# Three-term features kept in the gates' operand tiles, the power written later, one half of a relu written earlier

## The chip, the cores and the metric

The kernel runs on one core of one Trainium2 chip. The metric is the device time of one execution in microseconds (us); the median of several executions is compared. One core has five engines with an instruction queue each, which work through their queues in order and wait for each other through semaphores: TensorE (PE; its weight loads are shown apart as PEld), VectorE (DVE), ScalarE (ACT), GpSimd (POOL) and SyncE (SP). Transfers between HBM and SBUF run on 16 DMA engines; SyncE, ScalarE and GpSimd issue them.

## What is computed

A stack of four graph layers over N = 3327 nodes with D = 64 features and one weighted adjacency matrix `adj` (3327 x 3327, float32). `LN` is a layer norm over the features without scale or bias, and each layer is added to x:

```
h = relu(LN(x))
x = x + relu(ggc(relu(ggc(h, adj)), adj))        # layer 0: two gated graph cells (GRU)
h = relu(LN(x))
x = x + (W_rank @ (h @ w1) + b1)                 # layer 1
h = relu(LN(x))
x = x + three hops of  (adj*adj) @ . @ W.T + b   # layer 2
h = relu(LN(x))
x = x + two hops of  tanh([adj @ x, x] @ W)      # layer 3

ggc(x, adj):  m = adj @ (x @ W); gi = m @ wih.T + bih; gh = x @ whh.T + bhh
              r = sigmoid(i_r + h_r); z = sigmoid(i_z + h_z); n = tanh(i_n + r * h_n)
              return (1 - z) * n + z * x

W_rank: mask = adj != 0; rank = cumsum(mask, axis=1); deg = rank[:, -1:]
        k = min(deg, 100); pos = rank - (deg - k); W_rank = mask * 0.5 ** (k - pos) where pos > 0
```

So there are eight propagations through the adjacency matrix, numbered k = 0 to 7: two plain ones (k = 0, 1), one with the ranked weights (k = 2), three with squared entries (k = 3, 4, 5) and two plain ones (k = 6, 7).

## The kernel before

**Tiling.** The nodes are padded to 26 blocks of 128. The transposed matrix is read in tiles: one block of 128 source nodes (q = 0 to 25) against a group of target columns. There are two groups, `GROUPS` (L56): group 0 has the chunks 0 and 1 (384 columns each, in two halves s = 0, 1 of the node range), group 1 the chunks 2 and 3 (384 and 512 columns). A tile is 768 KB for group 0 and 896 KB for group 1 and lands in one of `NBUF` = 20 slots (L119). The sums of a chunk gather in PSUM over 26 source blocks.

**Units.** The work is a list of units (k, c, t): propagation k, target chunk c, tile t. `joint` (L615) lists two successive propagations of one group together, so that most tiles are loaded once for both. The order is k = 0 of group 0; k = 0 and 1 of group 1; k = 1 and 2 of group 0; k = 2 and 3 of group 1; and so on. Between the tiles of k = 0 stand counting units, which sum the mask of a tile over the rows (L496).

**The written order.** All engines follow the order in which the program emits their instructions. `run` (L667) goes through the units. For unit i it first emits loads as far ahead as slots are free (`dead`, a first-in first-out list; a load stops when only `RESERVE` = 3 are left), then prepares masks and squares some units ahead (`PREPARE`, L76), expands units up to i + 3 (`expand`, L444: for k = 2 two pairs of matmuls L270, then L474 on VectorE or L476 on ScalarE), then emits pieces of masks (L426 on VectorE; with the first half also the row DMA L431 on GpSimd), then the matmuls of unit i (`propagate`, L533, matmuls L561). Work that follows a finished chunk is written as generators. Each `yield` of one names a number of us, and `spend` (L337) takes from it an estimate for each unit that was emitted (0.645 us for 384 columns of a plain unit; 0.32 and 0.48 us for the two parts of a ranked one); when nothing is left, the generator runs on to its next `yield`. These are places in an order and not waits. `finish` (L329) runs a generator to its end at once; `propagate` calls it where the features of a source chunk are wanted and `y[k][cs]` isn't set yet (L551).

**The parts that the change touches.**
- `layernorm_relu` (L761): L766 to L768 on VectorE, a yield, L773 to L775, the power L776 on GpSimd (variance to the power -0.5), a yield of 2.5, and L780 on VectorE, which writes the features h.
- `before_0` (L868) uses it for the first features. It is advanced by hand before `run` (L972): each of the four chunks is begun and advanced twice, in the order 0, 0, 1, 0, 1, 2, 1, 2, 3, 2, 3, 3. At its end y[0][c] is set; after a further yield the features are transposed (L739).
- `gru` (L796): `both[c]` is a tile of 1 KB a partition and block that holds, for the two halves s, features in one half of the partitions and messages in the other, as the operand of the gates' matmuls (L807). L832 to L834 on VectorE make the new state d. In cell 0 its relu goes back into `both`, one half of the partitions by ScalarE (L837), the other by VectorE (L838). Matmuls L722 then bring it back to nodes (`stacked_to_nodes`), and a copy L881 makes y[1][c].
- `in_three` (L844) splits the features of k = 2 into three bfloat16 terms (L856 on ScalarE, L858 on VectorE), 0.75 KB a partition and block. They lie in a slot taken for each group: `parts[1]` when the first chunk of group 1 comes, `parts[0]` at the first chunk of group 0. The slots come back at L566 and L573. Four small DMAs (L865, on GpSimd) put the last row of each block into `lasty`.

Between the cell of k = 1 and the end of k = 5, where features are written into it anew, nothing reads `both[c]`.

Of the kernel before, what the change touches and what calls it, by code (L numbers as in the profile page):

```python
# [10 lines left out]
BF16 = mybir.dt.bfloat16  # L11
I16 = mybir.dt.int16
AF = mybir.ActivationFunctionType
ALU = mybir.AluOpType
# [30 lines left out]
N, D = 3327, 64  # L45
P = 128
NB = 13
# [5 lines left out]
NC = 4  # L53
PARTS = (4, 5)
CWM = 512
GROUPS = [(0, 1), (2, 3)]  # L56
# [14 lines left out]
PLAIN, RANKED, SQUARED = range(3)  # L71
KIND = [PLAIN, PLAIN, RANKED, SQUARED, SQUARED, SQUARED, PLAIN, PLAIN]
# [6 lines left out]
SPECIAL = None  # L79
# [3 lines left out]
def chunk_of(b):  # L83
    return next(c for c, (b0, b1) in enumerate(CH[:NC]) if b0 <= b < b1)


def sources_of(*chunks):
    return [s * NB + b for c in chunks for s in range(2) for b in range(*CH[c])]


def upper(n):
    return slice(n * D, (n + 1) * D)
# [3 lines left out]
def kernel(  # L96
# [9 lines left out]
    nc = tc.nc  # L106
# [12 lines left out]
    slots = [const.tile([P, 2, GWM], F32, name=f"adj{i}") for i in range(NBUF)]  # L119
# [7 lines left out]
    both = [const.tile([P, 2, (b1 - b0) * P], F32, name=f"both{c}") for c, (b0, b1) in enumerate(CH[:NC])]  # L127
# [131 lines left out]
    def blocks(c):  # L259
        return CH[c][1] - CH[c][0]  # L260

    def width(c):
        return blocks(c) * P
# [39 lines left out]
    def groups(t):  # L303
        return t.rearrange("p b s d -> p (b s) d")
# [24 lines left out]
    def finish(c):  # L329
        while c in tasks:  # L330
            advance(c)
# [5 lines left out]
    def spend(us):  # L337

        for c in list(tasks):
            if c in tasks and c not in running:  # L340
                tasks[c][1] -= us
                if tasks[c][1] <= 0:
                    advance(c)
# [6 lines left out]
    dead = deque(range(NBUF))  # L350
# [129 lines left out]
            t.mask.free()  # L480
        return wide.bitcast(BF16)

    ranks_left = set(sources_of(*GROUPS[0]))
    counts = {}
    squared = {}

# [46 lines left out]
    def propagate(k, c, t, rhs, first, last):  # L533
        if k == COUNT:
            count(t, first, last)
            return
        w = width(c)
        if first:
            sums[k, c] = [take(sums=True) for _ in range(2 if k == 7 and c == PARTS[1] else 1)]
            sums[k, c] = [sums[k, c][0], sums[k, c][-1]]  # L540
        acc = sums[k, c]
        if t is SPECIAL:
            for ch in range(NC):
                if ch != c:
                    finish(ch)
            terms = [[lasty[:, h, i, :] for h in range(2)] for i in range(3)]
            rhs = [rhs, rhs]
        else:
            s, b = divmod(t.q, NB)
            cs = chunk_of(b)  # L550
            if y[k][cs] is None:  # L551
                finish(cs)
            terms = [[yk[:, b - CH[cs][0], s, :]] * 2 for yk in (y[k][cs] if KIND[k] == RANKED else [y[k][cs]])]
            rhs = [rhs[:, h, :] for h in range(2)]
            if KIND[k] != RANKED:
                t.used()
            if (k, c, t) in squared:
                squared.pop((k, c, t)).free()
        for n, yq in enumerate(terms):
            for h in range(2):  # L560
                nc.tensor.matmul(acc[h][1][h * D:(h + 1) * D, :w], yq[h], rhs[h], start=first and n == 0,  # L561
                                 stop=last and n == len(terms) - 1)
        if KIND[k] == RANKED and c == NC - 1 and t is not SPECIAL and chunk_of(t.q % NB) in GROUPS[0]:
            ranks_left.discard(t.q)
            if not ranks_left:
                dead.append(parts[0])  # L566
        if t is not SPECIAL and t.early and t.mask is None:
            make_mask(t, RANKED)
        spend(STREAM_US * w / CWM * (0.75 if KIND[k] == RANKED else 1.0))
        if last:  # L570
            begin(c, after[k](c, sums.pop((k, c))))
            if KIND[k] == RANKED and c == NC - 1:
                dead.append(parts[1])  # L573

    units = []

# [184 lines left out]
    def layernorm_relu(h, c, scale=None, pace=1.0, squares_on_scalar=False):  # L761
        n = 2 * blocks(c)
        v = groups(xchunk(c))
        st = work.tile([P, 4, 8], F32, name="st", bufs=4)
        xc = work.tile([P, 8, D], F32, name="t2")
        nc.vector.tensor_reduce(st[:, 0, :n], v, AX.X, ALU.add)  # L766
        nc.vector.tensor_scalar(st[:, 1, :n], st[:, 0, :n], 1.0 / D, None, op0=ALU.mult)
        nc.vector.tensor_tensor(xc[:, :n], v, st[:, 1, :n, None].to_broadcast([P, n, D]), ALU.subtract)  # L768
        yield 1.5 * pace
        if squares_on_scalar:  # L770
            nc.scalar.activation(groups(h), xc[:, :n], AF.Square)
        else:
            nc.vector.tensor_tensor(groups(h), xc[:, :n], xc[:, :n], ALU.mult)  # L773
        nc.vector.tensor_reduce(st[:, 2, :n], groups(h), AX.X, ALU.add)
        nc.vector.tensor_scalar(st[:, 2, :n], st[:, 2, :n], 1.0 / D, EPS, op0=ALU.mult, op1=ALU.add)  # L775
        nc.gpsimd.tensor_tensor(st[:, 3, :n], st[:, 2, :n], mhalf[:, :n], ALU.pow)  # L776
        yield 2.5 * pace
        if scale is not None:
            nc.vector.tensor_scalar(st[:, 3, :n], st[:, 3, :n], scale, None, op0=ALU.mult)
        nc.vector.scalar_tensor_tensor(groups(h), xc[:, :n], 0.0, st[:, 3, :n, None].to_broadcast([P, n, D]),  # L780
                                       op0=ALU.max, op1=ALU.mult)
# [14 lines left out]
    def gru(acc, c, bi, bh, cell, pace=1.0):  # L796

        w = width(c)
        evacuate_stacked(acc, c)
        yield 0.8 * pace  # L800
        at = dead.popleft()
        r, z, d = (slots[at].rearrange("p s w -> p (s w)")[:, i * CWM:i * CWM + w] for i in range(3))

        def gate(g):
            i, ps = take()
            for s in range(2):
                nc.tensor.matmul(ps[upper(1 - s), :w], cells[:, cell, s, g, :], both[c][:, s], start=True, stop=True)  # L807
            return i, ps

        for g, v in enumerate((r, z)):  # L810
            i, ps = gate(g)
            nc.scalar.activation(v, ps[:, :w], AF.Sigmoid, bias=bsum[:, cell, g:g + 1])
            give(i)
        nh = None if cell == 0 else gate(2)
        ni = gate(3)
        yield 1.0 * pace
        nc.vector.scalar_tensor_tensor(r, ahead[c] if nh is None else nh[1][:, :w], bcol[:, bh + 2:bh + 3], r,
                                       op0=ALU.add, op1=ALU.mult)
        nc.vector.tensor_tensor(r, r, ni[1][:, :w], ALU.add)
        give(ni[0])  # L820
        if nh is not None:
            give(nh[0])
        else:
            del ahead[c]
            if not any(ch in ahead for ch in GROUPS[c // 2]):
                rooms[c // 2].free()
        yield 1.0 * pace
        nc.scalar.activation(r, r, AF.Tanh, bias=bcol[:, bi + 2:bi + 3])
        yield 0.8 * pace
        for s in range(2):  # L830
            u = upper(1 - s)
            nc.vector.tensor_tensor(d[u], both[c][u, s], r[u], ALU.subtract)  # L832
        nc.vector.tensor_tensor(d, d, z, ALU.mult)
        nc.vector.tensor_tensor(d, d, r, ALU.add)  # L834
        yield 2.2 * pace
        if cell == 0:
            nc.scalar.activation(both[c][upper(1), 0], d[upper(1)], AF.Relu)  # L837
            nc.vector.tensor_scalar(both[c][upper(0), 1], d[upper(0)], 0.0, None, op0=ALU.max)  # L838
            yield 1.0 * pace
        return at, d  # L840

    parts = {}

    def in_three(h, c):  # L844

        g = c // 2
        if g not in parts:
            parts[g] = dead.popleft()
        n = blocks(c) * 2 * 3 * D
        first = 2 * 3 * D * blocks(GROUPS[g][0]) if c == GROUPS[g][1] else 0  # L850
        room = slots[parts[g]].bitcast(BF16).rearrange("p s w -> p (s w)")[:, first:first + n]
        room = room.rearrange("p (b s i d) -> p b s i d", s=2, i=3, d=D)
        terms = [room[:, :, :, i, :] for i in range(3)]
        for i in range(2):
            yield 0.8
            nc.scalar.copy(terms[i], h)  # L856
            yield 0.8
            nc.vector.tensor_tensor(terms[2] if i else h, h, terms[i], ALU.subtract)  # L858

        yield 1.5  # L860
        b0, b1 = CH[c]
        for s in range(2):
            for k in range(2):
                q = k * D + s * NB
                nc.gpsimd.dma_start(out=lasty[q + b0:q + b1, k], in_=room[P - 1:P, :, s])  # L865
        return terms
# [155 lines left out]
```

## Time and profile before

Three executions took 719.84, 720.03 and 720.97 us; the median is 720.03 us. One more execution was profiled.

| what | value |
|---|---|
| median of the runs | 720.03 us |
| profiled execution, its own time | 723.89 us |
| its span, first to last instruction | 722.1 us |
| TensorE busy | 690.7 us, 96% of the span |
| VectorE busy | 346.2 us, 48% |
| ScalarE busy | 264.3 us, 37% |
| GpSimd busy | 77.3 us, 11% |
| moved by DMA | 201.31 MB, 279 GB/s over the span |
| TensorE idle before its first matmul | 8.4 us |

The profile page gives the busy time of each engine, the span in 40 slices, the DMA queues, the chain of work that ended last, and groups of instructions by line of the kernel with the idle time before them and what ended it. Further views of the same trace list waits, the instructions of an engine in order of time, the chain in order of time, and the granted clock of TensorE. Matmul ends are modelled, so a TensorE that shows busy is not always at its peak rate.

### The profile page before, as it was taken

To read this page: it belongs to the slowest core of one execution; us is meant where nothing else is said; L and a number is where in the kernel's file an instruction comes from. 1 tells how busy PE (TensorE), PEld (TensorE's weight loads), DVE (VectorE), ACT (ScalarE), POOL (GpSimd) and SP (SyncE) were. 2 spreads that over 40 slices of the span, in tenths; PEclk is the share of its full clock that TensorE was granted. 3 is DMA by queue.
4 is the path that set the end of the run, shared out by engine and by line. 5 is a ranking of instruction groups with operands and counts; after the bars stand their busy time and mean duration, and the time that the engine had idled before them with its cause. 6 is when DMAs were issued, how large, how long until landed. Compare 5 with 4: busy or idle time off the path is not lost.

```text
span 722.1 us, 12647 instructions
## 1 busy us (share of the span) xinstructions
PE 690.7 (96%) x5128; PEld 347.6 (48%) x5128; DVE 346.2 (48%) x701; ACT 264.3 (37%) x402; POOL 77.3 (11%) x114
## 2 busy tenths in 40 slices
PE   4999899999999897989999999999999999999997
PEld 1645444565446585445534444334444444344464
DVE  6767636634987987638615101521063456005101
ACT  0104000302137665778899321850065700000101
POOL 3500000001380602112100000000010000000000
PEclk9999999999999999999999999999999999999999
DMA  9999994299595367562799829981997399927991
GB/s 349 401 385 406 405 391 145 63 375 374 181 315 210 114 225 237 184 227 97 260 336 386 314 88 397 405 319 40 366 382 263 111 382 406 406 110 250 400 402 44
DMA packets 68549, 201.31 MB, mean 279 GB/s; under 512 B 7228, under 2 KB 8228, under 8 KB 68492
## 3 DMA queue, kind: packets, MB, share of 16 engines
q1 hardware_dynamic: 65596, 199.46, 74.6%
q8 instruction: 40, 0.66, 0.4%
q10 hardware_dynamic: 720, 0.85, 0.3%
q0 software_dynamic: 2176, 0.20, 0.2%
q14 instruction: 17, 0.14, 0.0%
HBM read 199.45 MB, written 0.85 MB: 277 GB/s over the span
## 4 chain that ended last, share of the span: by engine, by line
PE 52%; ACT 4%; DMA 2%; DVE 1%; issue 1%; ACTq 0%
PE sum L561 48%; ACT adj L403 3%; PE temp L270 3%; DMA adj<-totals 1%; PE temp L722 1%; DVE adj L426 1%; DMA out<-xs 1%; DVE both L757 0%; ACT both L756 0%; DVE xs L955 0%; ACT t L701 0%; PE sum L270 0%; ACT t L952 0%; ACT e L476 0%; ACTq L957 0%
## 5 line engine op out<-in xcount | busy, mean ns | idle before, releaser
L561 PE MATMUL sum<-adj,y 128*64 128x384 f32 (+3 forms) x3016 | 535.2, 505 | 12.1 <-DVE y L773 8.4
L561 PEld LDWEIGHTS sum<-adj,y 128*64 128x64 f32 x3016 | 223.3, 138 | 267.5 <-issue 223.8
L403 ACT ACTIVATE adj<-adj 128x768 f32<-128x768 f32 (+1 forms) x173 | 141.9, 891 | 50.2 <-PE sum L561 24.8
L426 DVE TENSOR_SCALAR adj<-adj 128x768 bf16<-128x768 f32 (+3 forms) x208 | 115.6, 606 | 32.4 <-PE temp L496 28.5
L476 ACT ACTIVATE e<-temp,bitsb 128x384 int16<-128x384 f32 (+1 forms) x114 | 65.4, 607 | 29.2 <-PE temp L270 16.1
L561 PE MATMUL sum<-e,adj 128*64 128x384 bf16 (+1 forms) x624 | 73.2, 341 | 0.6 <-DVE e L474 0.6
L757 DVE COPY both<-sum 64x384 f32<-64x384 f32 (+3 forms) x17 | 9.7, 568 | 117.1 <-ACT both L756 116.0
L756 ACT COPY both<-sum 64x384 f32<-64x384 f32 (+3 forms) x17 | 8.1, 478 | 154.8 <-PE sum L561 149.2
L270 PE MATMUL temp<-adj,tri 128*64 128x384 bf16 (+1 forms) x334 | 52.7, 348 | 8.7 <-DMA adj<-totals 5.4
L405 DVE TENSOR_TENSOR adj<-adj 128x768 f32<-128x768 f32 (+1 forms) x35 | 33.6, 1008 | 50.1 <-DMA adj<-in_adjT 29.6
L776 POOL TENSOR_TENSOR st<-st,mhalf 128x6 f32<-128x6 f32 (+1 forms) x16 | 24.5, 1531 | 295.5 <-DVE st L775 295.5
L561 PEld LDWEIGHTS <-adj 128*64 128x64 bf16 x624 | 40.3, 110 | 18.8 <-issue 6.7
L431 POOL DMA_DIRECT2D adj<-totals x52 | 31.4, 605 | 139.8 <-DVE adj L834 74.4
L474 DVE TENSOR_SCALAR e<-temp 128x384 int16<-128x384 f32 (+1 forms) x53 | 31.8, 607 | 26.3 <-issue 11.3
L270 PEld LDWEIGHTS <-tri 128*64 128x64 bf16 x416 | 28.9, 111 | 30.2 <-issue 13.7
L751 DVE STREAM_TRANSPOSE both<-y 32x96 f32<-32x96 f32 (+1 forms) x128 | 35.6, 278 | 2.9
L703 DVE COPY t<-sum 128x384 f32<-128x384 f32 x8 | 4.4, 555 | 62.2 <-PE sum L561 62.2
L496 PE MATMUL temp<-adj,behind 128*64 128x384 bf16 x208 | 29.1, 342 | 0.8 <-DVE adj L426 0.7
L496 PEld LDWEIGHTS <-behind 128*64 128x64 bf16 x208 | 14.1, 112 | 20.8 <-issue 18.6
L701 ACT COPY t<-sum 128x384 f32<-128x384 f32 (+1 forms) x8 | 4.2, 529 | 53.9 <-PE sum L561 53.9
L918 DVE TENSOR_TENSOR y<-temp,brow 128x384 f32<-128x384 f32 (+1 forms) x8 | 4.7, 592 | 29.6 <-PE temp L270 29.6
L530 ACT ACTIVATE lastw<-adj,bitsb 128x768 int16<-128x768 f32 (+1 forms) x2 | 2.0, 984 | 45.8 <-DVE adj L528 45.8
(121 smaller groups left out, 336.7 us busy)
## 6 DMA issues: line engine op xcount, KB each, us to landing
adj<-in_adjT SPq DMA_DIRECT2D x130, 768.0 KB, 8.7
adj<-in_adjT SPq DMA_DIRECT2D x104, 896.0 KB, 12.5
xs<-in_x SPq DMA_DIRECT2D x1, 640.0 KB, 4.0
adj<-totals POOLq DMA_DIRECT2D x26, 3.0 KB, 4.6
adj<-totals POOLq DMA_DIRECT2D x26, 3.5 KB, 3.1
out<-xs ACTq DMA_DIRECT2D x2, 192.0 KB
out<-xs ACTq DMA_DIRECT2D x1, 256.0 KB, 6.4
stage<-in_weights SPq DMA_DIRECT2D x2, 112.0 KB, 13.3
```

What stands on the lines that cost most here:

```text
L270: nc.tensor.matmul(out[hs], lhsT[:, hs], rhs, start=start, stop=stop)
L403: nc.scalar.activation(sq, v, AF.Square)
L405: nc.vector.tensor_tensor(sq, v, v, ALU.mult)
L426: nc.vector.tensor_scalar(t.mask.view[:rows, half], t.view()[:rows, half], 0.0, None, op0=ALU.not_equal)
L431: nc.gpsimd.dma_start(out=t.mask.view[P - 1:P], in_=totals[t.g][t.q:t.q + D + 1:D, :])
L474: nc.vector.tensor_scalar(wide[:, s], ps[:, :w], BITS, 0.0, op0=ALU.add, op1=ALU.max)
L476: nc.scalar.activation(wide[:, s], ps[:, :w], AF.Relu, bias=bitsb)
L496: nc.tensor.matmul(counts[c][1][s * D:(s + 1) * D, :w], behind[:, NQ - 1 - t.q:NQ - 1 - t.q + D], t.mask.view[:, s, t.cols(c)], start=firs ...
L561: nc.tensor.matmul(acc[h][1][h * D:(h + 1) * D, :w], yq[h], rhs[h], start=first and n == 0, stop=last and n == len(terms) - 1)
L751: nc.vector.transpose(to[at:at + 32, :, q], h[q * 32:(q + 1) * 32, :, s, f * 32:(f + 1) * 32])
L757: nc.vector.tensor_copy(both[c][upper(1), 1], acc[1][1][upper(1), :width(c)])
L776: nc.gpsimd.tensor_tensor(st[:, 3, :n], st[:, 2, :n], mhalf[:, :n], ALU.pow)
```

## The change

Three edits:
- **Terms in `both`.** `in_three` writes its three terms into `both[c]` in place of a slot. The two slots are no longer taken, and the code that gave them back is gone.
- **The power later.** In `layernorm_relu` a yield of 1.5 stands between L775 and the power, and one of 1.5 behind it, in place of 2.5 behind it alone. A layer norm thus has three yields, not two. The list that advances `before_0` by hand isn't changed.
- **Half of the relu at once.** In `gru`, cell 0, VectorE's half of the relu is written right behind L834, ahead of the yield; ScalarE's half stays behind it. The yield is 2.4 in place of 2.2.

```diff
-        if KIND[k] == RANKED and c == NC - 1 and t is not SPECIAL and chunk_of(t.q % NB) in GROUPS[0]:
-            ranks_left.discard(t.q)
-            if not ranks_left:
-                dead.append(parts[0])
...
             begin(c, after[k](c, sums.pop((k, c))))
-            if KIND[k] == RANKED and c == NC - 1:
-                dead.append(parts[1])
...
         nc.vector.tensor_scalar(st[:, 2, :n], st[:, 2, :n], 1.0 / D, EPS, op0=ALU.mult, op1=ALU.add)
+        yield 1.5 * pace
         nc.gpsimd.tensor_tensor(st[:, 3, :n], st[:, 2, :n], mhalf[:, :n], ALU.pow)
-        yield 2.5 * pace
+        yield 1.5 * pace
...
         nc.vector.tensor_tensor(d, d, r, ALU.add)
-        yield 2.2 * pace
+        if cell == 0:
+            nc.vector.tensor_scalar(both[c][upper(0), 1], d[upper(0)], 0.0, None, op0=ALU.max)
+        yield 2.4 * pace
         if cell == 0:
             nc.scalar.activation(both[c][upper(1), 0], d[upper(1)], AF.Relu)
-            nc.vector.tensor_scalar(both[c][upper(0), 1], d[upper(0)], 0.0, None, op0=ALU.max)
             yield 1.0 * pace
         return at, d
 
-    parts = {}
-
     def in_three(h, c):
 
-        g = c // 2
-        if g not in parts:
-            parts[g] = dead.popleft()
-        n = blocks(c) * 2 * 3 * D
-        first = 2 * 3 * D * blocks(GROUPS[g][0]) if c == GROUPS[g][1] else 0
-        room = slots[parts[g]].bitcast(BF16).rearrange("p s w -> p (s w)")[:, first:first + n]
+        room = both[c].bitcast(BF16).rearrange("p s w -> p (s w)")[:, :blocks(c) * 2 * 3 * D]
         room = room.rearrange("p (b s i d) -> p b s i d", s=2, i=3, d=D)
```

More of the change, by code (lines that the diff above doesn't have):

```diff
@@ L481, in expand @@
         return wide.bitcast(BF16)
-    ranks_left = set(sources_of(*GROUPS[0]))
     counts = {}
```

## The prediction

> **What bounds the kernel now.** I read the page first, then TensorE's waits, then for each long wait the instructions of the engine that it waited for. TensorE is the bound:
>
> ```profile
> PE 690.7 (96%) x5128; PEld 347.6 (48%) x5128; DVE 346.2 (48%) x701; ACT 264.3 (37%) x402; POOL 77.3 (11%) x114
> ```
>
> Only its 31.4 us of idle time (722.1 - 690.7) and what slows it can be won or lost. The view of waits for TensorE (who for whom: us, times, longest):
>
> ```profile
> PE sum L561 <- DVE y L773: 8.4, 1, 8.4
> PE temp L270 <- DMA adj<-totals: 5.4, 2, 3.3
> PE sum L561 <- DMA adj<-in_adjT: 2.8, 5, 1.4
> ...
> PE sum L722 <- DVE both L838: 2.1, 1, 2.1
> ```
>
> These four rows are the places that the change can reach: the start, two waits for a mask's last row, one for a tile, one for the relu. The start, VectorE in order of time:
>
> ```profile
> 3.17 0.55 DVE L766 TENSOR_REDUCE st<-xs 128x6 f32<-128x384 f32 x1 [3.17 <-DMA xs<-in_x]
> ...
> 4.56 0.56 DVE L773 TENSOR_TENSOR y<-t 128x384 f32<-128x384 f32 x1
> ...
> 5.82 0.55 DVE L766 TENSOR_REDUCE st<-xs 128x6 f32<-128x384 f32 x1
> ...
> 7.37 0.56 DVE L780 SCALAR_TENSOR_TENSOR y<-t,st 128x384 f32<-128x384 f32 x1 [0.21 <-POOL st L776]
> ```
>
> The first chunk's L780 starts at 7.37, and the first weight load follows 1.0 us later, at 8.37. VectorE around the relu:
>
> ```profile
> 71.76 0.56 DVE L834 TENSOR_TENSOR adj<-adj 128x384 f32<-128x384 f32 x1
> ...
> 76.18 0.34 DVE L838 TENSOR_SCALAR both<-adj 64x384 f32<-64x384 f32 x1
> ```
>
> The state is done at 72.32, but VectorE's half of the relu runs at 76.18, behind three mask pieces and the next chunk's state; TensorE, at L722 since 74.03, waits 2.13 us for it. GpSimd, and then the chain in order of time, around the two mask rows:
>
> ```profile
> 282.70 1.32 POOL L776 TENSOR_TENSOR st<-st,mhalf 128x6 f32<-128x6 f32 x1 [7.04 <-DVE st L775]
> 283.97 1.19 POOL L431 DMA_DIRECT2D adj<-totals  x2
> ```
> ```profile
> 283.97 4.42 DMA adj<-totals
> ...
> 317.10 5.18 DMA adj<-totals
> ```
>
> GpSimd sits in front of the power for 7.04 us; the row DMA behind it is issued at 283.97 and TensorE idles 3.33 us until it lands. The second row is issued only at 317.10 and costs 2.05 us.
>
> [...] The trace's clock record has three stretches at 0.5 of 3.41 us each, from 77.27, 288.89 and 323.02, right behind the waits of 2.13, 3.33 and 2.05 us[...], and none behind the tile wait of 1.36 us at 213.59. So a removed wait of 2 us or more brings 3.41 / 2 = 1.7 us beside itself. [...] a mask row issued at 291.32 with no tile on the way lands in 1.6 us, the two above in 4.4 and 5.2 us.
>
> **The change part by part.**
>
> *The start (the later power).* `before_0` now needs four advances to set y[0][c] and gets three. So before `run` VectorE gets L766 to L775 of all four chunks and no L780; the first unit finds y[0][0] unset, finishes the generator, and emits L780 and the six transposes L739 of chunk 0 ahead of its matmuls. VectorE: from 3.17, the first half (L766 to L768) takes 4.56 - 3.17 = 1.39 and the second (L773 to L775) 5.82 - 4.56 = 1.26, three times 2.65 = 7.95; the 512-wide chunk takes 1.64 + 1.52 by its own rows. L780 starts at 3.17 + 7.95 + 3.16 = 14.3, TensorE at 15.3: **6.9 us later**. Part of it comes back, since TensorE waits for tiles there: weight loads of successive tiles start at 42.80, 44.76, 46.68, 48.64, 50.63 and 52.56, 1.96 us apart, against 1.29 for 8 matmul records at 0.161 plus 0.32 for four counting ones. From 8.40 to 53.91 are 45.5 us; the work in it is 23 tiles x 1.29 = 29.7, 17 counts x 0.32 = 5.5, transposes 2.8, small matmuls 1.0, and 1.9 for the cold clock of the first 3.9 us: 40.9. The other 4.6 us are waits that a late TensorE doesn't have, its tiles having come meanwhile (loads don't wait for it: 17 tiles are issued by 26.6). 15.3 + 40.9 = 56.2 against 53.9, rounded up since it only just catches the last tiles: **+2.5** (bounds +1.5, and +6.9 if nothing comes back).
>
> *Relu at once.* L838 runs at 72.35. It adds nothing, but puts chunk 1's state 0.34 later. The wait of 2.13 and its 1.7 go; TensorE then comes to chunk 1's L722 at about 75.9, and ScalarE's half of it is done at 76.2: 0.3 back. **-3.5** (bounds -1.5, -3.8). The yield of 2.4 leaves chunks 0, 1 and 3 in the same unit; chunk 2 goes one unit later, and its copy L881 then meets the unit that reads it: at most 0.2.
>
> *The slots.* No slot is taken at chunk 2's L780, so each load of group 0's tiles 3 to 18 is issued at the place of the one before it. SyncE's issues were 202.20, 204.68 and 206.31 for the last three; the last now goes at 204.68, 1.6 us earlier, and lands when the one before it did, before TensorE's idle time began at 212.23. **-1.3** (bounds 0, -1.4). From the second slot on loads run two tiles ahead, but each still waits for the same slot to be read out, so they go at the same times. One place differs: the mask of tile 7 had the returned `parts[0]`; now it takes the slot that the load at 310.28 took. Its row goes at 310.3 in place of 308.14, and lands, 4 us later, before the 315.2 at which TensorE wants it; I put 0.3 on that. That load at 310.28 falls away (the tile is on its way already), and the row of 317.10 meets two tiles issued at 312.13 and 313.67, not three: 2.3 us less (896 KB at 406 GB/s), so it lands at about 320, when TensorE wants it (320.27). The wait of 2.05 falls to about 0.3 and the half clock with it: **-3.4** (bounds 0, -3.75).
>
> *The power at k = 2.* In group 0's second chunk L775 is emitted with unit (2,2,2) and the power 1.5 us of units later, with (2,2,13); the row DMA of tile 3 comes with the unit after next, (2,2,14), still behind it. GpSimd is held until 282.6 as before: **0** for the 3.33 us wait. Ahead of earlier powers some row DMAs and the clearing L518 now go first, but TensorE waited for none of them. L780 and the splits come one or two units later; VectorE is full from 231 to 250, and the same work passes through it: 0 (bounds -0.7, +0.7). The terms are read in the same shape from `both`: 0.
>
> *Sum.* +2.5 - 3.5 - 1.3 - 3.4 + 0.5 = -5.2, on a profiled span of 722.1, with 1.8 around it in that execution's 723.89. The runs' median is 3.9 below that execution; I take the same difference from it: 720.03 - 5.2 = **714.8 us**.
>
> **Rivals.**
> - *The slots win one wait of the two* (the tile, not the row: the row's slot is read out at 316.6 as before, and if its DMA still takes 5.2 us nothing is won): 714.8 + 3.4 = 718.2. *Neither*: 719.5.
> - *The start costs all of its 6.9*: if the late TensorE meets the tiles just the same. Against it, the 1.96 us pitch is a wait for tiles. 719.2.
> - *Relu moves the wait*: VectorE is full from 60 to 78, and the next chunk's half becomes the wait: -1.5 in place of -3.5, 716.8.
> - *The power does get behind the row of tile 3*, and the change does what its words say: 3.3 + 1.7 less, 709.8. Against it stands the count of units above.
> - *Slower: tiles ahead of rows.* If the deeper loads put one more tile of 2.3 us before each critical row: +2.3 at 288; tile 7's row, at 310.3 + 5.2 + 2.3 = 317.8, is 2.6 late plus 1.7; nothing won at 322. +2.5 - 3.5 - 1.3 + 2.3 + 4.3 + 0.5 = +4.8, 724.8. It decides once these rows cost over 3.5 us. For it, rows do wait behind tiles; against it, loads still follow slots.
>
> **How the numbers follow.** As summed 0.42; one slot wait alone 0.12; neither 0.08; full start 0.10; relu's wait moved 0.08; power past the row 0.10; slower 0.10. No change is within 0.2%, 1.4 us, about what these runs can tell: faster below 718.6, slower above 721.5. Faster: 0.42 + 0.12 + 0.08 + 0.10 = 0.72; same 0.08 + 0.10 = 0.18; slower 0.10. The range leaves out the two outermost cases, 0.10 each: 711.0 to 720.5; the likeliest alone has 712.5 to 717.
>
> **What would show it.** First matmul at about 15.3 and no tile waits before 55; no wait at L722 near 76 and no half clock there; no tile wait near 213; the wait at 288 still there, a power just before its row; no wait over 0.5 us near 320. A first matmul still at 8.4, a new wait for `totals` near 315, or a stretch at half clock that wasn't there would make it wrong.

## The result and the profile after

The changed kernel takes 718.04 us (median of 11 runs, 716.99 to 719.38) against 720.72 us for the kernel before beside it (11 runs). The medians are 2.7 us apart. The ratio on record, 0.9957 with a 95% interval of 0.9945 to 0.9970, is not that of these two medians; it makes 0.43%, 3.1 us (2.2 to 4.0). The forecast was 714.8 us and faster: the sign and the range (711.0 to 720.5) held, but the time lies outside the likeliest case's own range of 712.5 to 717: the gain came out at 3 us instead of 5.

The profiled executions say something else. Their spans are 722.1 us before and 716.2 us after, 5.9 us apart (5.2 were forecast on that scale). Why the profile shows nearly twice what the runs show is the main question below.

The changed kernel's page, first part (busy time of each engine):

```profile
PE 684.1 (96%) x5128; PEld 353.1 (49%) x5128; DVE 342.9 (48%) x700; ACT 265.3 (37%) x403; POOL 80.1 (11%) x114
```

TensorE is still the bound, with 32.1 us of idle time (716.2 - 684.1), 0.7 more than before. What fell is its busy time, by 6.6 us (690.7 to 684.1). Matmuls at half clock count as busy for longer here: before's L561 of 128x512 (f32) takes 1035 ns from 77.27 to 80.68 us, at a clock of 0.50, and 592 ns from 60 to 77. The three stretches at half clock of before, 3.41 us each, make 5.1 us of what fell. The changed kernel's trace has none of them ahead of its last matmul. Its waits after (in total, times, longest):

```profile
PE temp L732 <- DVE y L774: 15.0, 1, 15.0
PE temp L270 <- DMA adj<-totals: 3.1, 2, 2.5
...
PE sum L560 <- DMA adj<-in_adjT: 1.1, 1, 1.1
```

Against before, the start's wait grew from 8.4 to 15.0, the two waits for mask rows fell from 5.4 to 3.1, the tile waits from 2.8 to 1.1, and the relu's 2.1 is gone. The start in order of time, TensorE's row and then VectorE's:

```profile
14.96 1.55 PE L732 MATMUL temp<-ident,y 128*64 128x128 f32 x12 [14.96 <-DVE y L774]
```
```profile
14.36 1.49 DVE L774 SCALAR_TENSOR_TENSOR y<-t,st 128x384 f32<-128x384 f32 x3
```

All four chunks' first halves run first, and L774 (L780 before) is at 14.36, forecast at 14.3. VectorE around chunk 0's relu, and the one new wait behind it on TensorE:

```profile
74.24 0.56 DVE L828 TENSOR_TENSOR adj<-adj 128x384 f32<-128x384 f32 x1
74.84 0.35 DVE L830 TENSOR_SCALAR both<-adj 64x384 f32<-64x384 f32 x1
75.11 0.61 DVE L426 TENSOR_SCALAR adj<-adj 128x896 bf16<-128x896 f32 x1
```
```profile
79.04 0.32 PE L495 MATMUL temp<-adj,behind 128*64 128x384 bf16 x1 [0.52 <-DVE adj L426]
```

The relu's half now runs right behind the state, ahead of the mask pieces; TensorE meets one of these 0.52 us too early instead. GpSimd around the row near 288 us, and the two rows in the chain:

```profile
282.02 1.32 POOL L770 TENSOR_TENSOR st<-st,mhalf 128x6 f32<-128x6 f32 x1 [7.04 <-DVE st L768]
283.29 1.34 POOL L431 DMA_DIRECT2D adj<-totals  x2
```
```profile
283.29 3.55 DMA adj<-totals
...
314.28 3.75 DMA adj<-totals
```

The power is still just ahead of the row. But both rows land sooner than before (3.55 and 3.75 us against 4.42 and 5.18).

I matched the same matmuls of both traces and took the difference of their times, after minus before. Each stage's share, with the forecast of the sum beside it:

| place (us) | forecast | against the profile shown | against a second profile of before (e8) |
|---|---|---|---|
| start, to 60 | +2.5 | +2.5 | +2.2 |
| relu, 76 to 90 | -3.5 | -2.7 | -2.7 |
| tile wait, 130 | none | +0.9 | +0.3 |
| tile wait, 213 | -1.3 | -1.6 | -1.6 |
| VectorE full, 231 to 250 | 0 | +0.2 | +0.2 |
| mask row, 288 | 0 | -2.1 | -1.4 |
| mask row, 320 | -3.4 | -3.1 | -0.7 |
| small costs | +0.5 | in the others | in the others |
| span | -5.2 | -5.9 | -3.7 |

### The profile page after: what moved, and what is told of

It is laid out like the page before. It is cut to its first block, busy times and chain, and to the rows that moved or that the text cites. A ratio compares the mean times of both kernels' runs of the same rounds, so it can differ in the third digit from the quotient of the medians.

```text
span 716.2 us, 12638 instructions
## 1 busy us (share of the span) xinstructions
PE 684.1 (96%) x5128; PEld 353.1 (49%) x5128; DVE 342.9 (48%) x700; ACT 265.3 (37%) x403; POOL 80.1 (11%) x114
## 4 chain that ended last, share of the span: by engine, by line
PE 54%; DMA 3%; DVE 2%; ACT 1%; issue 0%; POOL 0%; ACTq 0%; DVEq 0%; SPq 0%; POOLq 0%
PE sum L560 50%; PE temp L270 3%; DMA adj<-totals 1%; PE temp L715 1%; DVE adj L426 1%; DMA adj<-in_adjT 1%; DMA out<-xs 1%; DVE both L750 0%; ACT both L749 0%; DVE e L474 0%; POOL st L770 0%; DVE xs L943 0%; PE sum L270 0%; ACT t L940 0%; ACT t L694 0%
## 5 line engine op out<-in xcount | busy, mean ns | idle before, releaser
L560 PEld LDWEIGHTS sum<-adj,y 128*64 128x64 f32 x3016 | 228.8, 137 | 249.4 <-issue 224.1
L426 DVE TENSOR_SCALAR adj<-adj 128x768 bf16<-128x768 f32 (+3 forms) x208 | 113.0, 594 | 38.7 <-PE temp L495 34.8
L560 PE MATMUL sum<-e,both 128*64 128x384 bf16 (+1 forms) x624 | 72.7, 339 | 0.6 <-DVE e L474 0.6
L560 PEld LDWEIGHTS <-both 128*64 128x64 bf16 x624 | 40.4, 110 | 18.5 <-issue 6.4
L495 PEld LDWEIGHTS <-behind 128*64 128x64 bf16 x208 | 16.8, 110 | 17.7 <-issue 16.5
```

The lines of the kernel that those rows point to most:

```text
L426: nc.vector.tensor_scalar(t.mask.view[:rows, half], t.view()[:rows, half], 0.0, None, op0=ALU.not_equal)
L495: nc.tensor.matmul(counts[c][1][s * D:(s + 1) * D, :w], behind[:, NQ - 1 - t.q:NQ - 1 - t.q + D], t.mask.view[:, s, t.cols(c)], start=firs ...
```

## The experiments

**One edit at a time.** Four kernels: the change without its cost at the start (e1), and the kernel before with the relu's (e2), the slots' (e3) or the power's edit alone (e4).

e1, the changed kernel with the first layer norm's power early:

```
     def layernorm_relu(..., early=False):
-        yield 1.5 * pace
+        if not early:
+            yield 1.5 * pace
         nc.gpsimd.tensor_tensor(st[:, 3, :n], ..., ALU.pow)
-        yield 1.5 * pace
+        yield (2.5 if early else 1.5) * pace
     def before_0(c):
-        yield from layernorm_relu(h, c)
+        yield from layernorm_relu(h, c, early=True)
```

> The changed kernel with the power of the first layer norm (before_0 alone) put back right behind L768 and its operands' half, as before. Theory (the later power costs the start 2.5 us, after 4.6 us of tile waits have paid the rest): the first matmul is back at 8.4 us, the tile waits before 55 us are back, and the span is 2.5 us under the changed kernel's 716.2, about 713.7; as a ratio to the kernel before about 0.992. Rival (what the start loses is won back later by waits for tiles in the second sweep): the span stays within 0.7 us of 716.2, ratio 0.9957 as for the change.

> The kernel before with the relu's edit alone. Theory: the wait of 2.1 us and the half-clock stretch near 76 us are gone, about 0.7 us of new waits for a mask piece near 79 us come, and all later records stand 2.7 us earlier than in the kernel before, if the other stretches at half clock are as there; ratio about 0.9965, and nearer 0.998 if the stretch at half clock belongs only to some executions. Rival (the time is given back at a tile wait before 213 us): the difference is gone by then, ratio 0.999 or more.

> The kernel before with the slots' edit alone (features in the idle place, two slots freed). Theory: the tile wait of 1.36 us near 213 us is gone (1.3 to 1.6 us), and the row near 320 us is issued 3 us earlier, so that its wait of 2.05 us falls to about 0.6 us (1.4 us, and 1.7 more where the half clock followed it): in all 3 to 4.7 us, ratio 0.994 to 0.996. The wait at 288 us shows which edit shortened it in the changed kernel: if this kernel has it at about 2.4 us it was this edit, if at 3.3 us it was another or none. Rival (free slots only move the loads, which meet at the next queue): ratio 0.998 or more.

> The kernel before with the later power alone. Theory: the first matmul is at 15 to 16 us, the first sweep ends 2.5 us later, no other wait changes by more than 0.3 us, the wait near 288 us is 3.3 us as before: 2.5 us slower, ratio 1.0035. Rival (the power gets behind the mask rows of k=2): the wait near 288 us falls by 1 us or more, and the ratio is at or below 1.001.

| kernel | median us | ratio to before | 95% interval | span |
|---|---|---|---|---|
| e1, start early | 715.82 | 0.9926 | 0.9901 to 0.9951 | 713.9 |
| e2, relu only | 719.18 | 0.9978 | 0.9964 to 0.9992 | 716.9 |
| e3, slots only | 717.77 | 0.9951 | 0.9936 to 0.9966 | 715.9 |
| e4, power only | 722.52 | 1.0016 | 1.0003 to 1.0028 | 720.4 |

The ratios are to the kernel before beside each run, whose median was 721.74 us for e1 to e4 (59 runs), 721.50 for e5 to e7 (43), 722.05 for e9 and e10 (13) and 721.28 for e11 and e12 (9). Times of different rounds are best compared by the ratio.

The start: e1 begins its matmuls at 8.75 us, is 1.9 us ahead of the change at 60 us and 2.25 at the end (2.2 in the medians, and by the ratios); e4 stands 2.3 us behind e8 (the kernel before, below) at 60 us. The theory's 2.5 about holds, and the rival (the cost is won back later) falls. That tile waits pay for the rest is to be seen at TensorE's weight loads. Between 8.4 and 58 us they wait for tiles in before and in e1 (the two lines of waits, in this order), and not at all in the changed kernel and in e4:

```profile
PEld sum L561 <- DMA adj<-in_adjT: 6.3, 13, 1.1
```
```profile
PEld sum L560 <- DMA adj<-in_adjT: 6.0, 15, 0.8
```

Only part of this shows as idle time of the matmuls (2.0 us in before from 8.4 to 55), since matmuls still run while a weight load waits.

The relu: e2 has the wait at L722 gone and a new 0.52 us near 77, as expected; the mean clock of its 22 runs is 0.9969, against 0.9958 for the 59 of before beside them. The slots: e3 has no wait near 213 and 0.62 us at the row near 318, and is the largest gain of the three. The power: e4 is slower, as expected. But its 0.16% is half of the 0.35% expected, its tile wait near 213 is 0.34 us where 1.36 was expected (against e8, 1.1 of the 2.3 us come back there), and its row near 288 waits 2.36 us, not 3.3. The three edits alone add up to 0.55%, and the whole change has 0.43%; the intervals allow both to be the same.

That last number is in all of them: 2.34, 2.46, 1.94 and 2.36 us near 288, whichever edit they have. So no edit shortened this wait; the profile of before had a long one.

**The kernel before again (e8)**, unchanged, one profile.

> The kernel before, unchanged, profiled once more. Theory (the 3.33 us near 288 us, and the 0.35 us near 130 us, are what that one execution had, not what the kernel has): this profile shows about 2.4 us near 288 us, about 1 us near 130 us, the stretches at half clock in other places or fewer of them, and a span 1 to 2 us under 722.1. Rival (the waits are the kernel's): 3.3 us near 288 us and half a microsecond or less near 130 us again, span within 0.7 us of 722.1.

It took 721.82 us, span 719.9. Its waits of TensorE:

```profile
PE sum L561 <- DMA adj<-in_adjT: 3.9, 6, 1.4
PE temp L270 <- DMA adj<-totals: 3.8, 2, 2.5
...
PE sum L722 <- DVE both L838: 2.1, 1, 2.1
```

The theory holds: 2.48 us near 288 (3.33 in the first profile), 1.31 at the next row (2.05), 0.99 near 130 (0.35), a span 2.2 us lower. Two stretches at half clock lie inside the matmuls, not three: the mean clock is 0.84 from 70 to 80 us and 0.89 from 280 to 295, but 1.00 from 315 to 327, where the first profile has 0.86. Measured against this profile the change gains 3.7 us, near the runs' 3.1; 3.4 of it is the two stretches (1.7 us each).

**Which slot.** e6 and e7 are the slots' edit alone, with one of the two slots taken and returned as before, and used for nothing.

```
     def in_three(h, c):
+        if c // 2 == 0 and 0 not in parts:      # e7: 1 in place of 0
+            parts[0] = dead.popleft()
...
+        if KIND[k] == RANKED and c == NC - 1 and t is not SPECIAL and chunk_of(t.q % NB) in GROUPS[0]:
+            ranks_left.discard(t.q)
+            if not ranks_left:
+                dead.append(parts[0])           # e7: parts[1], after k=2's last unit
```

> The kernel of the slots' edit alone (e3), but a slot is taken at chunk 2's L780 of k=1 and returned after group 0's last ranked tile, as before; it is used for nothing. Theory (both waits come from this slot): the tile wait of 1 to 1.4 us near 213 us is back, and the row near 320 us waits 1.4 to 2 us again: span 2.5 us over e3's 715.9, 718.4, ratio about 0.9985. Rival (the second slot or the place of the features does it): the waits stay as in e3, ratio about 0.995.

> The kernel of the slots' edit alone (e3), but the slot of the second group is taken as before and returned at the end of k=2; it is used for nothing. Theory (the second slot has no wait of its own): no wait near 213 us, 0.6 us at the row near 318 us, span within 0.7 us of e3's 715.9, ratio about 0.995. Rival (the row near 320 us comes earlier because of the second slot): its wait is 1.4 us or more again, span 1 us or more over e3's.

The expectation of e6 names the wrong chunk. The slot that e6 holds is group 0's, which is taken second, and the one that chunk 2's L780 takes first is group 1's, held in e7. Read by what they hold:

- e6 (group 0's slot held): 718.65 us, ratio 0.9967 (0.9952 to 0.9981). No wait near 213; 1.43 us at the row near 317.
- e7 (group 1's slot held): 719.61 us, ratio 0.9976 (0.9964 to 0.9988). 0.38 us of tile wait near 213; 1.11 us at the row near 319.

So the theory, that one slot makes both waits, falls: the tile wait belongs to the slot taken at chunk 2's L780. It is there in all five profiles that have this slot taken (1.36, 1.42, 0.99, 0.34 and 0.38 us) and in none of the nine that have not. The row near 320 has to do with the other slot. The two rows in the chain of e6, and then of e7:

```profile
281.45 3.85 DMA adj<-totals
312.74 4.57 DMA adj<-totals
```
```profile
283.53 3.70 DMA adj<-totals
314.66 4.25 DMA adj<-totals
```

In every trace the second row is issued 3.17 to 3.18 us before TensorE wants it; no edit moves that. Its wait is its landing time less 3.17. With group 0's slot taken, a load of SyncE's goes out 6.82 us ahead of the row, beside those at 4.97 and 3.42 us ahead, and the row lands in 4.44 to 5.18 us (five profiles, mean 4.7: before 5.18, e4 4.80, e6 4.57, e2 4.50, e8 4.44). Without that load it lands in 3.52 to 4.25 (nine profiles, mean 3.8; e7 4.25, the changed kernel and e3 3.75, e5 3.59, e1 3.52). One tile less on the way was worth 0.9 us to this row.

**The row ahead of the power (e5)**: e1 with the power of group 0's layer norms of k=2 held back by 3.5 us of units instead of 1.5.

```
-            yield 1.5 * pace
+            yield hold * pace          # 1.5, and 3.5 for the layer norms of k = 2 of group 0
         nc.gpsimd.tensor_tensor(st[:, 3, :n], ..., ALU.pow)
```

> The kernel of e1 with one more edit: in group 0's layer norms of k=2 the power comes 3.5 steps behind its operands' half, not 1.5, which puts one mask row (L431) of group 1 ahead of chunk 1's power on GpSimd; no other engine's order changes but a few of VectorE's mask pieces. Theory (the row waits for the power, and TensorE for the row): the row is issued at least 1.3 us earlier than in e1 (281.4 us there) and the wait of 2.34 us falls to 1.0 or less: span 712.5, ratio about 0.991. Rival (the row cannot be issued earlier, since the row before it or its tile is what is late): the wait stays over 2 us, or comes back as a wait for chunk 1's operands, span within 0.5 us of e1's 713.9.

713.54 us, ratio 0.9889 (0.9868 to 0.9910), span 711.2. GpSimd in order of time, in e1 and then in e5:

```profile
280.12 1.32 POOL L771 TENSOR_TENSOR st<-st,mhalf 128x6 f32<-128x6 f32 x1 [7.04 <-DVE st L768]
281.39 1.34 POOL L431 DMA_DIRECT2D adj<-totals  x2
```
```profile
270.79 1.35 POOL L771 TENSOR_TENSOR st<-st,mhalf 128x6 f32<-128x6 f32 x1 [21.46 <-DVE st L768]
272.11 0.64 POOL L431 DMA_DIRECT2D adj<-totals  x1
279.18 1.35 POOL L771 TENSOR_TENSOR st<-st,mhalf 128x6 f32<-128x6 f32 x1 [6.43 <-DVE st L768]
280.50 0.60 POOL L431 DMA_DIRECT2D adj<-totals  x1
```

The first of the two rows that stood behind the second power goes out at 272.11, some 8 us earlier once the 0.9 us by which e5 is ahead there are taken off. It lands at 277.56, and the 2.34 us wait is gone; two waits of under 0.2 us for mask pieces are left. The theory holds, and the rival (nothing earlier, or a new wait) falls: the span is 2.7 us under e1's, 1.8 of it at this row (the other 0.9 lies at the start and near 130 us, where the two kernels are the same), and the median 2.3. This is the fastest of all kernels here, 1.1% under the kernel before.

**When a wait brings half clock.** The prediction put 1.7 us of half clock on each wait of 2 us or more. In the traces that doesn't hold: the same wait of 2.13 us at L722 is followed by a stretch in the first profile of before (0.50 from 77.27) and in e8 (0.84 on the mean from 70 to 80 us), and not in e6. The changed kernel's 2.46 us near 288 is followed by none (1.00 from 289.36 to 292.77), the first profile's 2.05 us near 320 by one (0.50 from 323.02). Here is e6 at its wait. The columns are the part of the span and its length, the busy time of TensorE, its weight loads, VectorE, ScalarE and GpSimd (instructions in brackets), the granted clock, the DMA share and GB/s:

```profile
75.28:78.69 3.41, 1.71 (x28) 1.09 (x30) 3.41 (x8) 0.52 (x1) 0.00 (x0) 1.00 1.03 408
78.69:82.11 3.42, 3.42 (x46) 1.92 (x44) 2.60 (x6) 0.00 (x0) 0.00 (x0) 1.00 1.03 403
```

TensorE idles for 1.70 us of the first line, and for the wait's other 0.43 us ahead of it; the clock stays at 1.00. To see how often the wait brings a stretch I used e5 with the relu's edit undone, so that this is its only wait over 2 us (e9; e11 is the same once more). Then VectorE's half of chunk 0's relu is written five times (e10) and three times (e12), with the same values, which lengthens the wait. The shares of executions behind the numbers of "Theory" below are an estimate of mine, which these runs do not show. "Theory" of e11 is that e9's six runs were luck.

```
-            nc.vector.tensor_scalar(both[c][upper(0), 1], d[upper(0)], 0.0, None, op0=ALU.max)
+            for _ in range(5 if c == 0 else 1):        # e12: 3
+                nc.vector.tensor_scalar(both[c][upper(0), 1], d[upper(0)], 0.0, None, op0=ALU.max)
```

> The kernel of e5 with the relu's edit undone, so that one wait of 2.13 us (L722 near 76 us) is its only wait over 2 us. [...] Theory [...] the mean granted clock over the runs shows 0.5 stretches (0.0024 each) more than e5's 0.9990, so 0.9979, and the time is 1.1 + 0.5 x 1.7 = 1.9 us over e5's, 715.5. Rival (a wait of over 2 us always brings the stretch, as the prediction had it): one stretch more in every run, mean clock 0.9966, 2.8 us over e5, 716.3.

> e9 with VectorE's half of chunk 0's relu written five times instead of once (the same values), so that the wait near 76 us grows by 4 x 0.34 to about 3.5 us. Theory [...] 0.4 stretches more than e9 in the mean clock, about 0.9970, and 1.36 + 0.4 x 1.7 = 2.0 us over e9, 717.5. Rival (always): the same clock as e9, and 1.36 us over it.

> The kernel of e9 once more, because its six runs had no stretch at half clock more than e5's (mean clock 0.9990 both), which a share of 48% would do in 2 of 100 cases. Theory [...]: mean clock about 0.9979 and some 0.8 us over e9's 714.9. Rival [...]: mean clock 0.9987 or more, 714.9 again.

> e10 with three writes instead of five: the wait near 76 us is about 2.9 us. Theory [...] mean clock between e9's and e10's, 0.9973 to 0.9980, and 0.8 us of wait plus 1.2 us of slow clock over e9's trace without a stretch: 716.5. Rival [...]: mean clock 0.999 and 715.7.

| kernel | wait near 76 | median us | ratio to before | mean clock over the runs |
|---|---|---|---|---|
| e5 | none | 713.54 | 0.9889 | 0.9990 (6 runs) |
| e9 | 2.13 | 714.91 | 0.9919 | 0.9990 (6) |
| e11 | 2.13 | 714.95 | 0.9918 | 0.9986 (5) |
| e12 | 2.91 | 717.36 | 0.9945 | 0.9984 (5) |
| e10 | 3.68 | 718.13 | 0.9951 | 0.9969 (8) |

e11's profile has the stretch. The same two lines, to be held against those of e6:

```profile
74.52:77.94 3.42, 1.29 (x25) 0.90 (x26) 3.38 (x9) 0.52 (x1) 0.00 (x0) 1.00 1.03 406
77.94:81.35 3.41, 3.41 (x34) 2.25 (x32) 1.57 (x5) 0.00 (x0) 0.00 (x0) 0.50 1.03 405
```

Here the whole 2.13 us (3.42 - 1.29) fall in the first line, and the clock is 0.50 in the second. e9's profile, the same kernel with the same wait, stays at 1.00 from 72.26 to 82.50. What makes the difference between two executions isn't shown.

"Always" falls: e9's runs show nothing of a stretch in each (mean clock 0.9990, as in e5). But the share also came out lower than forecast: of the eleven runs of e9 and e11 two stand out (716.62 and 716.37 us, clock 0.998 and 0.996; the others are 714.3 to 715.5), where 48% were forecast. Two of e5's six runs, which have no such wait, have 0.998 too. e2 says otherwise: it lacks this wait, and its clock is above that of before by 0.0011, 0.46 of a stretch. e10's clock is as forecast (0.9969); e12's (0.9984) is between theory and rival, but its 717.36 us is above both forecasts (716.5 and 715.7). Its two runs with a clock of 1.000 took 716.3 and 716.9 us, against 714.3 to 715.5 for the nine others of e9 and e11; the longer wait explains 0.8 us of that, and the rest is open. So the runs with the longest wait (3.68 us) have more half clock (0.9969, against 0.9990 and 0.9986 at 2.13 us), and the rate at 2.1 us stays open.

## Why the prediction was right or wrong

**The start: right.** The first matmul was forecast at 15.3 and is at 14.96, and 2.5 us of net cost were forecast against 2.2 to 2.5. That the tile waits pay for the rest is shown by e1 and e4: against before, the changed kernel's TensorE is 7.9 us late at 10 us and 2.5 at 60, and its weight loads no longer wait for tiles. In e4's runs the later power costs 1.2 us (0.2 to 2.0) in all.

**The relu: right in the mechanism, too large.** The forecast of -3.5 was 2.13 of wait and 1.7 of half clock, less 0.3 given back. Given back are about 1.1, for the mask piece at 79.04 (0.52) and the next one (0.21), and other small delays. Where neither kernel has the half clock (e2 against e6), the edit is worth only 1.0 us. The runs of e2 say 0.22%, 1.6 us (0.6 to 2.6): the 1.0, and 0.8 for the half stretch that its clock gains.

**The tile wait near 213: right**, by the slot that I had named (e6 against e7). 1.3 was forecast and 1.6 went; the five profiles that have the wait have 0.34 to 1.42, on average 0.9, so 1.6 is much for it.

**The mask row near 320: right in the mechanism, wrong in its size.** The load at 310.28 falls away, as forecast. I let the row land 2.3 us sooner for that; the two profiles have 1.4 and the means over all profiles 0.9. The rest of the -3.4 was a half clock that, of the two profiles of before, only the first had: against e8, the wait goes from 1.31 to 0.62, and that is all. In the runs the slots' edit alone (e3) gives 3.5 us (2.5 to 4.6) of the 4.7 forecast for this row and the tile, and its clock of 0.9973 is 0.0015 above that of before: about one of the 3.5 is half clock. The changed kernel's 0.62 is a little over the 0.5 that was to show the forecast right.

**The mask row near 288: right that no edit moves it, wrong in the number.** The power stayed ahead of the row. The -2.1 us in the trace are one slow landing (4.42 us; 3.03 to 3.85 in the eight other traces with the row behind the power) and its half clock. That the power's place was the cause of the wait, e5 shows by moving it; what I had put at 5.0 us for that rival (714.8 to 709.8) is 1.8 in the trace.

**The tile wait near 130 (+0.9): not foreseen.** The profile of before had 0.35 us there, e8 has 0.99, and the changed kernel 1.14. It is no effect of the change.

**The step that failed is the last one**: "The runs' median is 3.9 below that execution; I take the same difference from it." The sum of -5.2 was near on the profile's scale (-5.9), in part by luck: the -2.1 at the row near 288, which no edit made, stands against a relu that gave 0.8 less and a tile wait of +0.9. And the profiled execution of before was no measure for the runs. It had three stretches at half clock and two slow rows; the changed kernel's has no stretch, and stands (718.06) on its median (718.04).

How many stretches the runs have can be read from the clock. Over the 102 runs of the kernel before beside e1 to e7 the mean clock is 0.996. One stretch of 3.41 us costs 3.41 x 0.5 / 720 = 0.0024 of it, so this is 1.7 stretches a run, not 3; the changed kernel's 0.9991 makes 0.4. Both counts are somewhat too high, since the record also counts half clock behind the last matmul (the changed kernel's trace shows a clock of 0.51 from 716.02 to 716.16, with no matmul from 712.60 on; e6's and e9's profiles have 0.999, less missing than one stretch takes, and e5, which has no such wait, has 0.9990 over its runs). Over the same 102 runs the time rises by some 1.7 us for each 0.0024 of clock, which agrees with 1.7 us for one stretch. Their median is 721.69 us: the profiled execution stood 2.2 us over it, which is the 1.3 stretches that it had too many. The other 1.7 of the 3.9 is that the three runs on which the forecast stood had a median of only 720.03.

The clocks of the runs of before beside the changed kernel are not on record, so the 102 stand for them. By this count, 1.3 x 1.7 = 2.2 us of the gain of 3.1 is clock, and about 1 us is what the waits gave after the start's cost. The runs with a clock of 0.999 or more say the same: nine of the changed kernel have a mean of 717.8 us, and eight of the 102 have 719.1. In the first profile of before, 5.1 of the 5.9 us are its three stretches. That the changed kernel's profile has none is luck as well: no stretch follows its wait of 2.46 us near 288, and two of its eleven runs have a clock of 0.997.

## What to carry to other kernels

Profile the kernel before twice, if its profiled execution stands over its median: what differs between the two profiles belongs to the execution, and a gain that is read from it isn't to be counted on. A removed wait of some 2 us on TensorE gave no more than its own length here (the relu's 2.13 us gave 1.0, as the next waits took the rest), plus 1.7 us in some share of the runs: count that share and not the whole, and look at the mean clock of the runs to know it. A small DMA that stands behind a waiting instruction on its queue can cost more than its own size: moving one mask row ahead of one power gave 1.8 us in the trace and 2.3 in the medians, not much less than the whole change.

## What the runs showed of the hardware

- The three stretches at half clock in the first profile of before are 3.41 us long each and follow waits of 2.13, 3.33 and 2.05 us. The length of the wait alone doesn't tell whether one follows: 2.13 us has one in before, e8 and e11 and none in e6 and e9, and 2.46 us has none in the changed kernel. In e10 the clock is 0.50 for 6.83 us in one piece, from 76.83 to 83.66, and TensorE still idles for 1.48 us of it, of a wait of 3.68 us (one profile):

```profile
76.83:80.24 3.41, 1.93 (x22) 1.36 (x24) 3.21 (x8) 0.00 (x0) 0.00 (x0) 0.50 1.03 407
80.24:83.66 3.42, 3.42 (x34) 2.18 (x32) 0.67 (x3) 0.00 (x0) 0.00 (x0) 0.50 1.03 403
```

- The same row DMA, issued 1.13 us ahead of its use behind the same loads, landed in 3.4 to 4.4 us from one execution to the next (before, e1, e2, e4, e6, e7, e8 and the changed kernel). With TensorE waiting for it, that alone is a microsecond of the kernel's time.
